# Edge blocks taken singly, and the last chunk's dense layers split at the nodes of the last two blocks

## The chip, the cores and the metric

The kernel runs on one core of a Trainium2 chip. The metric is the device time of one execution in microseconds. Five engines work beside each other, each through its own list in order: TensorE (PE; its weight loads are shown as PEld), VectorE (DVE), ScalarE (ACT), GpSimd (POOL) and SyncE (SP), which issues most of the plain transfers.

## The reference

A graph layer over 8,192 nodes with 256 channels and 131,072 edges, all in float32; the edges are sorted by their destination.

```python
ea = edge_attr @ w_e + b_e                       # 131072 x 64 @ 64 x 256
msg = relu(x[src] + ea)                          # gather of rows of x
agg = segment_sum(msg, dst, num_segments=8192)
t = x + agg
h_local = bn1(relu(t @ w1 + b1) @ w2 + b2 + x)
# attention of 4 heads within groups of 32 nodes, on x alone
h_attn = bn2(attention(x) @ out_w.T + out_b + x)
out = h_local + h_attn
out = out + relu(out @ m_w1 + m_b1) @ m_w2 + m_b2
result = layernorm(x + bn3(out))
```

The attention does not need the edges. The dense layers of a node need the sums of all edges that end in it.

## The kernel before, in words

**Edges.** The edges go in 128 blocks (NB) of 1,024. For a block, `gather` (L157) issues eight indirect transfers on POOL, each fetching 128 rows of x into a tile xs; there are four xs buffers. `edge_products` (L208, with the bias at L203 for the first 20 blocks) multiplies the edge attributes by w_e on PE. `edge_messages` adds both on DVE (L229) and applies relu on ACT (L233); the addition frees the xs buffer. `edge_hot` (L241) makes one-hot rows on DVE. `edge_sums` (L255) multiplies the one-hot rows by the messages, which gives the sums over a window of 32 nodes for each of four groups h of a block, each in its own 32 rows of the PSUM tile pw; they are copied to the tile ws (L265; for the last block L262 on DVE and L263 on ACT). `edge_place` (L280) multiplies ws by a second one-hot matrix, which puts the sums at their nodes in the PSUM tile l2, and DVE adds l2 to the transposed nodes xT (L289). The tiles pw and l2 share one buffer.

A block's window begins at node b x 64 minus a slack and is 64 nodes plus twice the slack wide; the slack is 24 at block 125 and 16 at blocks 126 and 127.

**Nodes.** The nodes go in 16 chunks of 512. `attention_front` and `attention_back` (L434 to L529) do the attention, with q and k at L445, scores at L476, the product with bd at L514 and the output projection at L526. `dense` does the four dense layers through its helper `layer` (L545), evacuated at L552 (w1, ACT), L555 (w2, DVE), L561 (m_w1, ACT) and L570 (m_w2, DVE), then transposes back (L582), adds x (L585), normalizes (L587 to L595) and stores (L598). A whole chunk's layers are 512 columns wide. The last two chunks go in parts: chunk 14 in two of 256, chunk 15 as 256, 128 and 128, each part with its own bound on which blocks must have been placed.

**Order.** PE's list is the order in which the program is written. A loop takes two blocks at a time up to block 103 (TAIL = 104): products and messages of the first, sums of the pair before, products and messages of the second, then the placement, and between them `work.run(us)`, which takes steps from four streams of node work (attention back and front, two of dense), each step with a planned cost, until its budget of 4.2 us (5.1 from block 20) a block is used up. A stream's entry may start when its condition holds; for dense this is `summed`: all blocks that reach into its nodes are placed. Up to block 25 the lists of DVE and ACT are in program order too; behind that a scheduler orders them. From block 104 on, a planner goes by times: `came` is when a block's gathers should have landed, and at each point it writes down whatever is due first of placement, sums, products, messages or a step of node work.

Of the kernel before, what the change touches and what calls it, by code (L numbers as in the profile page):

```python
# [72 lines left out]
def gnn_kernel(ctx: ExitStack, tc: tile.TileContext, x, src, dst, edge_attr, w, out):  # L73
# [173 lines left out]

    def edge_sums(blocks):

        pw = pps.tile([P, 2, C], FP, name="pw", tag="pw", bufs=1)  # L250
        for i, b in enumerate(blocks):
            msg, oh = msg_of.pop(b), oh_of.pop(b)
            turns = [(h, j) for j in range(TJ) for h in range(NH)]
            for h, j in sorted(turns) if b == NB - 1 else turns:
                nc.tensor.matmul(  # L255
                    pw[h * WN : (h + 1) * WN, i, :], oh[:, h * TJ + j, :], msg[:, h, j, :],
                    start=(j == 0), stop=(j == TJ - 1), skip_group_check=True,
                )
        n = len(blocks)
        ws = epool.tile([P, 2, C], FP, name="ws", tag="ws", bufs=2)  # L260
        if blocks[-1] == NB - 1:
            nc.vector.tensor_copy(ws[:, :n, :P], pw[:, :n, :P])  # L262
            nc.scalar.copy(ws[:, :n, P:], pw[:, :n, P:])  # L263
        else:
            newest["ws"] = nc.scalar.copy(ws[:, :n], pw[:, :n]).ins  # L265
        oh2 = epool.tile([P, 2, WB], FP, name="oh2", tag="oh2")
        for i, b in enumerate(blocks):
            wn = window(b)
            nc.vector.tensor_scalar(oh2[:, i, :wn], iota_n[:, :wn], wrow[:, b : b + 1], None, ALU.is_equal)
        return blocks, ws, oh2  # L270

    def edge_place(blocks, ws, oh2):
# [4 lines left out]
        for i, b in enumerate(blocks):  # L277
            at, wn = first_node(b) - n, window(b)
            for k in range(KC):
                nc.tensor.matmul(  # L280
                    l2[:, k, at : at + wn], ws[:, i, k * P : (k + 1) * P], oh2[:, i, :wn],
                    start=(i == 0 and k == 0), stop=(i == last), skip_group_check=True,
                )
# [250 lines left out]

    def dense(n0, st, pool, bank, t_a=0, t_z=TN, own=("h1", "m1", "zT", "y", "")):

        assert st["done"]
        nt = t_z - t_a
        cs, ts, part = slice(t_a * P, t_z * P), slice(t_a, t_z), nt / TN
        xn, tT, hA = st["xn"][:, ts, :], st["xT"][:, :, cs], st["hA"][:, :, cs]  # L540

        def layer(wt, nk, o, act):
            ps = bank()[:, : nt * P]
            for k in range(nk):
                nc.tensor.matmul(  # L545
                    ps, wt[:, k, o * P : (o + 1) * P], act[:, k, :], start=(k == 0), stop=(k == nk - 1)
                )
            return ps

        h1 = pool.tile([P, KC, nt * P], FP, name="h1", tag=own[0])  # L550
        for o in range(KC):
            nc.scalar.activation(h1[:, o, :], layer(w1, KC, o, tT), AF.Relu, bias=v_("b1", o))  # L552
            yield 1.7 * part
        for o in range(KC):
# [3 lines left out]
            yield 1.7 * part  # L558
        m1 = pool.tile([P, 2 * KC, nt * P], FP, name="m1", tag=own[1])
        for o in range(2 * KC):  # L560
            nc.scalar.activation(m1[:, o, :], layer(mw1, KC, o, hA), AF.Relu, bias=v_("m_b1", o))  # L561
            yield 1.7 * part
        zT = pool.tile([P, KC, nt * P], FP, name="zT", tag=own[2])
        for o in range(KC):

            nc.scalar.activation(
                zT[:, o, :], hA[:, o, :], AF.Identity, scale=s3[:, o : o + 1], bias=c3[:, o : o + 1]
            )
        for o in range(KC):
            nc.vector.scalar_tensor_tensor(  # L570
                zT[:, o, :], layer(mw2, 2 * KC, o, m1), s3[:, o : o + 1], zT[:, o, :], op0=ALU.mult, op1=ALU.add
            )
            yield 3.4 * part
        y = pool.tile([P, nt, C], FP, name="y", tag=own[3])
        st6 = pool.tile([P, TN, 6], FP, name="st", tag="st" + own[4])
        mv = pool.tile([P, TN, 2], FP, name="mv", tag="mv" + own[4])
        for t2 in range(0, nt, 2):
            n2 = min(2, nt - t2)
            ps = bank()[:, : n2 * C].rearrange("p (t c) -> p t c", t=n2)
            for t in range(n2):  # L580
                for k in range(KC):
                    nc.tensor.transpose(  # L582
                        ps[:, t, k * P : (k + 1) * P], zT[:, k, (t2 + t) * P : (t2 + t + 1) * P], ident
                    )
            nc.vector.tensor_add(y[:, t2 : t2 + n2, :], ps, xn[:, t2 : t2 + n2, :])  # L585
        for t in range(nt):
            nc.vector.bn_stats(st6[:, t, :], y[:, t, :])  # L587
            nc.vector.bn_aggr(mv[:, t, :], st6[:, t, :])
        rstd = pool.tile([P, TN], FP, name="rstd", tag="rstd" + own[4])
        nc.scalar.activation(rstd[:, :nt], mv[:, :nt, 1], AF.Sqrt, bias=eps_t)  # L590
        st["dense"] = t_z == TN
        yield 0.9 * part
        nc.vector.reciprocal(rstd[:, :nt], rstd[:, :nt])
        for t in range(nt):
            nc.vector.tensor_scalar(  # L595
                y[:, t, :], y[:, t, :], mv[:, t, 0:1], rstd[:, t : t + 1], ALU.subtract, ALU.mult
            )
        nc.sync.dma_start(out[ds(n0 + t_a * P, nt * P), :].rearrange("(t p) c -> p t c", p=P), y)  # L598
        yield 0.0
# [100 lines left out]
    with tc.manual_schedule(engines={PE}):  # L700

        def last_of(c, t_z=TN):

            return max(b for b in range(NB) if first_node(b) < c * CH + t_z * P)

        def summed(c, t_z=TN):
            last = last_of(c, t_z)
            return lambda: placed >= last and chunk[c].get("done") and not xp_of and b > 2

        for c in range(NCH):  # L710
# [11 lines left out]
            if c < NCH - 2:  # L722
                work.add(DENSE, summed(c), dense(c * CH, st, npool, bank))
        for i, c, t_a, t_z in (
            (DENSE2, NCH - 2, 0, 2), (DENSE, NCH - 2, 2, 4), (DENSE2, NCH - 1, 0, 2), (DENSE, NCH - 1, 2, 3),
            (DENSE2, NCH - 1, 3, 4),
        ):
            d = dense(c * CH, chunk[c], npool, bank, t_a, t_z, *([OTHER] if i == DENSE2 else []))
            ready = summed(c, t_z)
            if i == DENSE2:  # L730
                ready = lambda r=ready: r() and chunk[NCH - 1].get("done")
            work.add(i, ready, d)
# [5 lines left out]
        b = 0  # L738
        while b < TAIL:
            if b == NV:  # L740
                early.close()
                stated[0] = False
            blocks, per = range(b, b + 2), 2 * (PER_X if b < NX else PER)
            copying[0] = copy_stream(b // 2 - 1)
            for i in blocks:
                if i + 2 < NB:
                    gather(i + 2)
                if 4 <= i < 8:
                    wt, name = ((w1, "w1"), (w2, "w2"), (mw1, "m_w1"), (mw2, "m_w2"))[i - 4]
                    nc.sync.dma_start(wt, w[name].rearrange("(k p) m -> p k m", p=P))  # L750

            if b:
                edge_products(b)
                edge_messages(b)
                next_edges(b + 2)
            if waiting:
                sums = edge_sums(waiting)
            waiting = list(blocks)
            if not stated[0]:
                work.run(0.2 * per)  # L760
            edge_products(b + 1)
            edge_messages(b + 1)
            next_edges(b + 3)
            if stated[0]:
                for i in blocks:
                    edge_hot(i)
                    copy_some(2)
            work.run((0.3 if stated[0] else 0.1) * per)
            copy_load(b // 2)
            if sums:  # L770
                edge_place(*sums)
                placed, sums = sums[0][-1], None
            work.run(0.2 * per)
            if not stated[0]:
                for i in blocks:
                    edge_hot(i)
            work.run(0.5 * per)
            copy_some(4 * TN)
            b += 2

        came = [7.9 + 10.035 * (i + 1) for i in range(NB)]
        t, p, m, s, l = came[b - 2] + 20, b, b, b - 2, b - 2
        added = dict((i, came[i] + 2.0) for i in range(b))
        summed_at, bank_free = {}, t
        work.at = [t] * len(work.streams)
        while l < NB:
# [4 lines left out]
            elif s < m:  # L791
                times[1] = max(added[s] + 1.2, bank_free)
            if p < NB and m == p:
                times[2] = added[p - 1]
            if m < p:
                times[3] = came[m]
            if t >= times[0]:
# [3 lines left out]
                bank_free = work.placed_at = t + 0.7  # L801
                l += 1
            elif t >= times[1]:
                sums = edge_sums([s])
                t += 1.2
                summed_at[s] = t
# [146 lines left out]
```

## Time and profile before

| what | value |
|---|---|
| median of 3 runs | 1314.89 us (1314.71 to 1315.25) |
| profiled execution, whole | 1315.3 us |
| its span, first to last instruction | 1313.3 us |
| granted TensorE clock, mean | 0.959 |
| busy: PE, DVE, ACT, POOL | 1196.5, 800.9, 589.2, 976.1 us |
| rows of PE | 7,635 |
| gathers (L157) from x, from the copy xb | 160, 864 |

The profile is a page and a trace of one execution. In a group's row the numbers stand for: count, busy time in us, mean ns of one instruction, idle time of the engine just before them and what ended most of it. A timeline row gives start, length, engine, line, operation, tiles, shape and count. A wait's row gives who waited for whom, us in total, how often, and the longest. In a row of busy time by stretches, each engine's busy us is followed by the number of its instructions, and at the end stand granted clock, DMA share and GB/s.

### The profile page before, as it was taken

The numbers are of one execution on the slowest core, as the hardware profiler recorded it, in microseconds if no ns is written. First come the engines' busy times: TensorE is split into PE (matmuls) and PEld (weight loads), VectorE is DVE, ScalarE is ACT, GpSimd is POOL, SyncE is SP. The second block draws the span as 40 slices with busy tenths as digits, with TensorE's granted clock in tenths as the row PEclk, the third lists the DMA queues.
The fourth block names the chain that finished last, engine by engine and source line by source line (L and its number), as shares of the span: only waits on it lengthen the run. The fifth ranks groups of instructions, "written<-read, shape, count | busy, mean of one in ns | idle before, by whom it ended". The sixth has DMA issues, their size and how long they took to land.

```text
span 1313.3 us, 20960 instructions
## 1 busy us (share of the span) xinstructions
PE 1196.5 (91%) x7635; PEld 720.4 (55%) x7635; DVE 800.9 (61%) x1629; ACT 589.2 (45%) x841; POOL 976.1 (74%) x1032
## 2 busy tenths in 40 slices
PE   4987989999999989898997998989898999989987
PEld 3554655556555655554554554545556555555655
DVE  5567665756666565745646574565647558475754
ACT  2524443454545363544544444353454445444433
POOL 6777777777777777777777777777777777777772
PEclk8988999999999989998998998989898999999989
DMA  9999876677766665755757566576567567655742
GB/s 234 283 338 273 263 210 175 172 183 193 177 170 170 169 183 162 195 155 157 194 157 185 154 185 168 154 186 170 170 169 189 149 169 193 162 162 161 193 129 58
DMA packets 148905, 240.34 MB, mean 183 GB/s; under 512 B 27934, under 2 KB 112188, under 8 KB 148028
## 3 DMA queue, kind: packets, MB, share of 16 engines
q0 software_dynamic: 49152, 134.28, 38.0%
q1 hardware_dynamic: 98556, 104.65, 29.5%
q8 instruction: 62, 1.02, 0.3%
q14 instruction: 47, 0.39, 0.1%
q10 hardware_dynamic: 1088, 0.00, 0.0%
HBM read 222.06 MB, written 16.78 MB: 182 GB/s over the span
## 4 chain that ended last, share of the span: by engine, by line
PE 49%; POOL 20%; issue 10%; DMA 9%; DVE 7%; ACT 4%; SPq 0%; DVEq 0%; POOLq 0%; ACTq 0%
POOL xs L157 20%; PE at L545 13%; PE pe L208 10%; PE at L445 6%; DMA xs<-xb,srci 5%; PE pw L255 5%; PE at L526 3%; PE l L280 3%; PE pe L203 2%; DVE msg L229 2%; PE at L459 2%; DMA xs<-in_x_dram,srci 2%; PE at L514 1%; ACT pr L486 1%; DVE bd L506 1%
## 5 line engine op out<-in xcount | busy, mean ns | idle before, releaser
L157 POOL DMA_INDIRECT xs<-xb,srci x864 | 820.7, 950 | 263.4 <-issue 245.1
L233 ACT ACTIVATE msg<-msg 128x1024 f32<-128x1024 f32 (+1 forms) x259 | 270.0, 1046 | 402.6 <-DVE msg L229 398.6
L229 DVE TENSOR_TENSOR msg<-pe,xs 128x1024 f32<-128x1024 f32 (+1 forms) x259 | 306.5, 1205 | 196.0 <-PE pe L208 75.8
L208 PE MATMUL pe<-we,eaT 64*128 64x256 f32 x2048 | 267.8, 398 | 17.0 <-ACT pr L486 11.8
L208 PEld LDWEIGHTS pe<-we,eaT 64*128 64x128 f32 x2048 | 193.6, 192 | 121.2 <-issue 62.7
L157 POOL DMA_INDIRECT xs<-in_x_dram,srci x144 | 138.3, 961 | 43.9 <-issue 39.9
L255 PE MATMUL pw<-msg,oh 128*32 128x256 f32 x2048 | 128.8, 384 | 1.4 <-ACT msg L233 1.0
L545 PE MATMUL at<-hA,mw 128*128 128x512 f32 (+2 forms) x304 | 124.8, 538 | 3.4 <-DVE hA L555 3.4
L445 PE MATMUL at<-xT,inT 128*128 128x512 f32 x256 | 121.9, 602 | 3.2 <-ACT xT L435 3.2
L545 PE MATMUL at<-m,mw 128*128 128x512 f32 (+2 forms) x304 | 119.0, 534 | 0.1
L190 DVE STREAM_TRANSPOSE eaT<-ea 128x512 f32<-128x512 f32 x128 | 89.9, 702 | 24.7 <-PE pe L208 20.7
L255 PEld LDWEIGHTS pw<-msg,oh 128*32 128x32 f32 x2048 | 59.5, 110 | 63.3 <-issue 22.9
L280 PEld LDWEIGHTS l<-oh,ws 128*128 128x128 f32 x512 | 74.4, 196 | 28.1 <-issue 20.9
L280 PE MATMUL l<-oh,ws 128*128 128x160 f32 (+4 forms) x512 | 86.3, 309 | 2.4 <-ACT ws L265 1.6
L545 PEld LDWEIGHTS at<-hA,mw 128*128 128x128 f32 x304 | 54.1, 192 | 51.6 <-issue 40.8
L545 PEld LDWEIGHTS at<-m,mw 128*128 128x128 f32 x304 | 54.6, 192 | 48.7 <-issue 44.9
L445 PEld LDWEIGHTS at<-xT,inT 128*128 128x128 f32 x256 | 46.9, 191 | 57.5 <-issue 48.3
L448 ACT ACTIVATE qk<-at,vec 128x512 f32<-128x512 f32 x64 | 43.9, 685 | 74.9 <-PE at L445 74.8
L545 PE MATMUL at<-xT,w 128*128 128x512 f32 (+2 forms) x152 | 68.5, 588 | 7.4 <-DVE xT L289 7.4
L545 PE MATMUL at<-h,w 128*128 128x512 f32 (+2 forms) x152 | 65.0, 550 | 9.6 <-ACT oT L521 6.3
L561 ACT ACTIVATE m<-at,vec 128x512 f32<-128x512 f32 (+2 forms) x76 | 46.8, 618 | 56.5 <-PE at L545 56.2
L570 DVE SCALAR_TENSOR_TENSOR zT<-at,s,zT 128x512 f32<-128x512 f32 (+2 forms) x38 | 25.1, 662 | 72.0 <-PE at L545 72.0
(113 smaller groups left out, 1228.3 us busy)
## 6 DMA issues: line engine op xcount, KB each, us to landing
ea<-in_edge_attr_dram SPq DMA_DIRECT2D x512, 128.0 KB
xs<-xb,srci POOLq DMA_INDIRECT x864
xn<-in_x_dram SPq DMA_DIRECT2D x16, 512.0 KB
out_dram<-y SPq DMA_DIRECT2D x14, 512.0 KB
xp<-in_x_dram SPq DMA_DIRECT2D x10, 512.0 KB
xb<-xp SPq DMA_DIRECT2D x10, 512.0 KB
xp<-in_x_dram SPq DMA_DIRECT2D x3, 1024.0 KB
xb<-xp SPq DMA_DIRECT2D x3, 1024.0 KB
```

Source lines behind the costliest of these rows:

```text
L157: nc.gpsimd.indirect_dma_start(out=xs[:, h, j, :], out_offset=None, in_=x if b < NX else xb[:, :], in_offset=bass.IndirectOffsetOnAxis(ap= ...
L190: nc.vector.transpose(eaT, ea[:, QR:].rearrange("p (g d) -> p g d", d=ED)[:, :, :QR])
L208: nc.tensor.matmul(pe[:, i, u, :], eaT[rows, h + u], we[rows, :], start=(b >= NX), stop=True, skip_group_check=True)
L229: nc.vector.tensor_add(msg[:, hs, js].rearrange("p u i c -> p i u c"), pe[:, js, u : u + n, :], xs[:, hs, js].rearrange("p u i c -> p i u c"),
L233: nc.scalar.activation(msg[:, hs, js], msg[:, hs, js], AF.Relu)
L255: nc.tensor.matmul(pw[h * WN : (h + 1) * WN, i, :], oh[:, h * TJ + j, :], msg[:, h, j, :], start=(j == 0), stop=(j == TJ - 1), skip_group_ ...
L280: nc.tensor.matmul(l2[:, k, at : at + wn], ws[:, i, k * P : (k + 1) * P], oh2[:, i, :wn], start=(i == 0 and k == 0), stop=(i == last), ski ...
L445: nc.tensor.matmul(ps, inT[:, k, o * P : (o + 1) * P], xT[:, k, :], start=(k == 0), stop=(k == KC - 1))
L448: nc.scalar.activation(qk[:, o, :], ps, AF.Identity, bias=v_("in_b", o))
L526: nc.tensor.matmul(ps, outT[:, k, o * P : (o + 1) * P], oT[:, k, :], start=(k == 0), stop=(k == KC - 1))
L545: nc.tensor.matmul(ps, wt[:, k, o * P : (o + 1) * P], act[:, k, :], start=(k == 0), stop=(k == nk - 1))
L561: nc.scalar.activation(m1[:, o, :], layer(mw1, KC, o, hA), AF.Relu, bias=v_("m_b1", o))
```

## The change

The loop up to block 103 takes one block at a time; sums and placement of a block come one block later, not one pair later. The first two blocks are still summed together. Budgets for node work are the same per block. The order within an iteration of the first 26 blocks is: products, messages, sums of the block before, one-hot rows, 0.3 of the budget, placement, 0.7 of the budget.

The last chunk's dense layers go in four parts: nodes 0 to 256, 256 to 368, 368 to 432 and 432 to 512 of the chunk. `dense` takes node bounds instead of tiles of 128; a part that doesn't start at a multiple of 128 loads its own rows of x into a tile xl.

The last block's sums are made in two steps: the first three groups (`first_sums`), and the fourth when its messages are there. Its two copies go to two tiles ws, one from DVE and one from ACT, instead of two halves of one.

```diff
+    def first_sums(b):
         pw = pps.tile([P, 2, C], FP, name="pw", tag="pw", bufs=1)
+        group_sums(pw, 0, b, [(h, j) for h in range(NH - 1) for j in range(TJ)])
+        return pw
...
+            group_sums(pw, 0, blocks[0], [(NH - 1, j) for j in range(TJ)])
+            for k, copy in enumerate((nc.vector.tensor_copy, nc.scalar.copy)):
+                half = epool.tile([P, 2, C], FP, name="ws", tag="ws", bufs=2)
+                copy(half[:, 0, :P], pw[:, 0, k * P : (k + 1) * P])
+                ws.append(half[:, :, :P])
...
-    def dense(n0, st, pool, bank, t_a=0, t_z=TN, own=("h1", "m1", "zT", "y", "")):
+    def dense(n0, st, pool, bank, a=0, z=CH, own=("h1", "m1", "zT", "y", "")):
+        if a % P:
+            xr = pool.tile([P, 1, C], FP, name="xl", tag="xl", bufs=2)
+            nc.sync.dma_start(xr[:w, 0, :], x[ds(n0 + a, w), :])
...
-            (DENSE2, NCH - 2, 0, 2), (DENSE, NCH - 2, 2, 4), (DENSE2, NCH - 1, 0, 2), (DENSE, NCH - 1, 2, 3),
-            (DENSE2, NCH - 1, 3, 4),
+        late, last = (first_node(b) % CH for b in (NB - 2, NB - 1))
+            (DENSE2, NCH - 2, 0, CH // 2), (DENSE, NCH - 2, CH // 2, CH), (DENSE2, NCH - 1, 0, CH // 2),
+            (DENSE, NCH - 1, CH // 2, late), (DENSE2, NCH - 1, late, last), (DENSE, NCH - 1, last, CH),
...
-        while b < TAIL:
-            blocks, per = range(b, b + 2), 2 * (PER_X if b < NX else PER)
+        for b in range(NV):
+            per = PER_X if b < NX else PER
+            gather(b + 2)
             if b:
                 edge_products(b)
                 edge_messages(b)
                 next_edges(b + 2)
-            if waiting:
+            if b > 1:
                 sums = edge_sums(waiting)
+                waiting = []
+            waiting.append(b)
+            edge_hot(b)
+            copy_some(2)
+            work.run(0.3 * per)
             if sums:
                 edge_place(*sums)
                 placed, sums = sums[0][-1], None
+            work.run(0.7 * per)
...
+        for b in range(NV, TAIL):
+            gather(b + 2)
+            edge_products(b)
+            edge_messages(b)
+            next_edges(b + 2)
+            sums = edge_sums(waiting)
+            waiting = [b]
+            work.run(0.3 * PER)
+            edge_place(*sums)
+            placed = sums[0][-1]
+            work.run(0.2 * PER)
+            edge_hot(b)
+            work.run(0.5 * PER)
...
-        t, p, m, s, l = came[b - 2] + 20, b, b, b - 2, b - 2
+        t, p, m, s, l = came[b - 2] + 20, b, b, b - 1, b - 1
...
+                if s == NB - 1:
+                    times[1] = max(came[s] - 0.4, bank_free) if first is None else came[s] + 1.2
...
+            elif t >= times[1] and s == NB - 1 and first is None:
+                first = first_sums(s)
+                t += 0.8
```

## The prediction

> **What bounds the kernel now.** I read the page's engine rows first: TensorE (PE) is busy for 91% of the span and GpSimd (POOL) for 74%, which seems to say PE. The waits of POOL correct that.
>
> ```profile
> POOL xs L157 <- issue: 292.2, 951, 2.6
> POOL xs L157 <- DMA xs<-xb,srci: 5.8, 19, 0.3
> ```
>
> All of POOL's gaps but one are 0.3 us; the 2.6 us one stands ahead of the first gather, and 0.30 + 0.95 us is simply what one indirect gather takes. The timeline of POOL gives the ends of the stream:
>
> ```profile
> 4.23 1.10 POOL L157 DMA_INDIRECT xs<-in_x_dram,srcd  x1 [2.63 <-issue]
> ...
> 1290.23 0.95 POOL L157 DMA_INDIRECT xs<-xb,srci  x1 [0.30 <-issue]
> ```
>
> 1,024 gathers from 4.23 to 1291.18 are 1.257 us each: POOL never waits for anybody. So nothing done to blocks 0 to 103 can shorten the kernel; it can only lengthen it, by making a gather wait for its buffer. What can be won lies behind the last gather: 1313.3 - 1291.2 = 22.1 us. That stretch I read in the chain that ended last and in the busy time by stretches:
>
> ```profile
> 1294.57 1.15 PE pw L255 x16
> 1296.39 0.70 PE l L280 x4
> 1297.11 0.34 DVE xT L289
> 1297.49 6.12 PE at L545 x52
> 1303.61 0.40 PE at L582 x2
> 1304.01 2.75 PE at L545 x24
> 1306.78 0.36 DVE zT L570
> 1307.18 0.34 PE at L582
> ```
>
> ```profile
> 1274.48:1289.43 14.95, 14.43 (x106) 10.61 (x105) 5.37 (x12) 6.51 (x11) 11.29 (x13) 1.00 0.37 106
> 1289.43:1297.49 8.06, 5.29 (x45) 3.96 (x45) 6.00 (x18) 4.55 (x12) 1.45 (x2) 1.00 0.25 79
> 1297.49:1307.50 10.01, 9.68 (x80) 9.06 (x80) 3.62 (x11) 4.36 (x12) 0.00 (x0) 1.00 0.05 15
> ```
>
> (PE's busy time is the second number.) PE is full from 1274.5 to 1289.4, has 2.8 us idle around the last two blocks, and is full again from 1297.5 to the end: at full clock (1.00) the dense layers of the last chunk, not the edge sums, set the end.
>
> **What a narrow pass costs.** The change makes the parts 256, 112, 64 and 80 nodes wide instead of 256, 128 and 128 (blocks 126 and 127 begin at nodes 8,048 and 8,112, that is 368 and 432 within the chunk). A float32 multiplication leaves two rows in the trace; I call them passes. The groups kept apart by shape show what width is worth (mean ns behind the comma):
>
> ```profile
> L280 PE MATMUL l<-oh,ws 128*128 128x160 f32 x320 | 56.3, 321 | 0.0
> L280 PE MATMUL l<-oh,ws 128*128 128x144 f32 x80 | 13.2, 298 | 0.0
> L280 PE MATMUL l<-oh,ws 128*128 128x128 f32 x56 | 8.6, 284 | 0.5 <-ACT ws L265 0.5
> L280 PE MATMUL l<-oh,ws 128*128 128x112 f32 x40 | 6.1, 282 | 1.1 <-ACT ws L265 1.1
> L280 PE MATMUL l<-oh,ws 128*128 128x96 f32 x16 | 2.4, 283 | 0.8 <-ACT ws L263 0.8
> ```
>
> From 160 to 128 columns a pass gets 37 ns shorter, from 128 to 96 only 1 ns. So there is a floor at about 128 columns. The spacing at 128 columns comes from runs in the timeline: 8 passes take 1.06 us and 4 take 0.61, so (1.06 - 0.61)/4 = 0.112 us a pass; at 256 it is 3.04/14 = 0.217. I price 112, 80 and 64 columns at 0.112 us (the last two are an extension of the flat rows). Bounds: 0.112 above; below, in proportion from the 256-column row, 0.053 for 64 and 0.068 for 80. I take the upper end, since the 96-column row is the nearest.
>
> The Trainium skill, "TensorE: Matmul & The Clock Gate", section "LDWEIGHTS (loading the stationary operand)", says that a weight load takes its columns divided by 1.2 in ns, whatever the rows: 107 ns for the 128 columns that all these passes have. By that rule the floor is 0.107 and the sum below would be 0.5 us smaller. Its section "Back-to-back issue gap" gives an isolated 64-column matmul some 60 cycles; the 96-column row above speaks against using that here; by it the time would be that of the rival on width.
>
> **The change, part by part.**
>
> *Blocks 0 to 103 singly.* Each block gets its own pw copy, placement and xT addition; matmuls stay the same in number, ACT gets 50 more copies of about 0.4 us and DVE as many more short additions, both on engines busy 45% and 61%. None of it reaches the end unless POOL stops. The closest call is block 14, whose additions free the buffer of block 18 (four xs buffers):
>
> ```profile
> 185.70 1.22 DVE L229 TENSOR_TENSOR msg<-pe,xs 128x1024 f32<-128x1024 f32 x1 [0.50 <-PE pe L208]
> 187.28 0.95 POOL L157 DMA_INDIRECT xs<-in_x_dram,srci  x1 [0.30 <-DVE xp L621]
> ```
>
> The addition ends at 186.92 and the 145th gather starts at 187.28: 0.4 us to spare (blocks 10, 16 and 18 have 3.5). PE's order in the changed program puts 3.0 us more ahead of block 14's products: one block's sums and placement (1.3) and two output multiplications (1.7). Five times before that block a placement follows its sums at once, and must wait for the copy behind both relus, ready 2.7 us after the products (68.88 to 71.71 less 0.2 for a half-wide copy around block 4) while the sums cover 0.9: 5 x 1.8 = 9 us. Against that, the attention's bd now stands a block ahead of its use in DVE's order, so PE's two long waits on it (6.35 us at 83.5, 3.3 behind block 13) should go, and the 5.46 us wait at 117.6, where DVE had a whole softmax between two blocks, should shrink. Sum: 3.0 + 9 - 9.65 = +2.4, down to -3.1 if the last goes too. Less the 0.4 to spare, POOL stops for 0 to 2.0 us; if no wait goes, up to 11.6. I take 0, and keep the rest as a rival. From block 26 on the spare time is 17 us or more, so nothing there counts.
>
> *A fourth part.* One part is 24 multiplications, 48 passes x 0.112 = 5.4 us of PE, and two more transposes, 0.2; the 112-column part costs what a 128-column one did. +5.6 us, in a stretch where PE had 2.8 us idle.
>
> *When the last placement comes.* Products of block 126 start at 1274.48, held by a gather's landing, as before. Until the placement of block 126 (1288.35 before) PE now also does both first layers of the 112 part, 16 passes = 1.8 us, and waits 0.6 us for the xT addition right behind the placement of block 125, where second-layer work stood before: about 1290.7. DVE's additions of block 127 stand behind that block's xT addition, so they start at 1291.65 instead of 1289.29, and run without gaps (0.6 us for each of three, 0.35 for each of two): the last relu ends near 1294.8 instead of 1293.89. The sums of the first three groups end at 1295.1, a pair of 112-column multiplications takes 0.45, and the last group starts at 1295.55. Here the split saves nothing: its four passes share one column group and follow each other, and the whole block's 16 passes took 1.09 us because four groups run side by side. They end at 1296.6. The two copies into separate tiles run side by side: 0.45 instead of 0.75 us. The placement starts at 1297.1 instead of 1296.39, +0.7. Bounds: 1295.5 (if nothing but the last relu holds it) and 1297.4.
>
> *Behind the last placement.* The program's order has 38 multiplications and 4 transposes there before, 60 (12, 24 and 24 of the three parts) and 6 after. The 80-column part's first layer, ready at the xT addition, stands behind 26 of them. 0.45 for the placement + 120 passes x 0.112 = 13.4 + 0.4 for four transposes + 0.7 for the last zT step (1306.47 to 1307.18 before) = 15.0 us, so the last transpose starts at 1312.1 instead of 1307.18: +4.9 us. Normalization and store behind it are the same (6.1 us). The three earlier stores and the two small xl loads ride on SP, which is idle enough.
>
> Sum: 1315.3 (the profiled execution, 2.0 over its span) + 4.9 = 1320.2; it stood 0.4 above the median, so **1319.7**. With the placement's bounds and half a microsecond of waits the forecast's own range is 1317.6 to 1320.5.
>
> **Rivals.**
> - *POOL stops in the first 26 blocks*, on top of the tail: for it the 0.4 us at block 14, against it the vanishing bd waits. 1 to 3 us more: 1321 to 1323; 1331 at the outside.
> - *Passes cost by width* (it isn't slower): 24 x 0.096 + 48 x 0.053 + 48 x 0.068 = 8.1 us behind the placement, against 76 x 0.112 = 8.5. What remains is the later placement (+0.7) and up to 1.4 us of waits, since layers this short no longer cover the 0.7 us from a pass to its evacuated tile: 1315.2 to 1317. It decides if a 64-column pass is under 0.08 us.
> - *PE's idle 2.8 us takes up half of the new part*: +1.5 to 2.5, about 1317.
> - *The change does what its parts are for* (placement at 1295.5 and passes by width, without waits): -1.3, 1313.6. Even this is within 0.2%.
>
> **Chances.** Forecast 0.55, POOL stop 0.22, width 0.14, idle 0.04, the rest, faster, 0.05. Slower by over 0.2% (2.6 us, about what a measurement of this kernel can tell from no change) 0.77; within 0.18; faster 0.05. The range reaches from the width rival to the POOL stop: 1316.0 to 1323.0.
>
> **What would show it.** POOL's waits: no gap over 0.3 us (else the first rival). 64- and 80-column rows of the dense line with a mean near 282 ns, as at 128. The last placement near 1297, and some 126 PE rows behind it without gaps. The prediction is wrong if those rows are clearly shorter, if the 80-column part's first layer is done before 1299, or if the span ends under 1315.

## The result, and the profile after

The changed kernel takes 1328.68 us (median of 4 runs, 1328.38 to 1332.66) against 1315.07 for the kernel before in the same comparison: ratio 1.011, 95% interval 1.009 to 1.0129. It is slower by 13.6 us; the prediction was 1319.7, with a range that ended at 1323.0.

The profiled execution has a span of 1326.5 us (1313.3 before), 13.2 more. The first place to look is where the gathers end. First POOL's waits, then its timeline at two places:

```profile
POOL xs L157 <- issue: 292.9, 954, 2.6
POOL xs L157 <- DVE msg L229: 10.3, 13, 6.1
```

```profile
176.26 0.95 POOL L157 DMA_INDIRECT xs<-in_x_dram,srci  x1 [0.30 <-issue]
183.34 0.94 POOL L157 DMA_INDIRECT xs<-in_x_dram,srci  x1 [6.13 <-DVE msg L229]
...
1296.20 0.95 POOL L157 DMA_INDIRECT xs<-xb,srci  x1 [0.30 <-issue]
```

A gap of 6.1 us stands where before had none over 0.3: the first gather of block 17 waits for the additions of block 13, which free its buffer. The last gather is done at 1297.15 instead of 1291.18: 6.0 us of the 13.2 are this stop (a second and short one, 0.78 us, follows ahead of block 18's first gather). The other 7.2 us lie behind the last gather (29.4 us instead of 22.1). The chain that ended last shows them from the last block's sums on:

```profile
1299.98 2.25 PE pw L250 x12
1302.22 0.63 PE at L562 x4
1302.85 0.99 PE pw L250 x4
...
1303.87 0.30 DVE ws L274
...
1304.19 0.28 ACT ws L274
...
1304.51 0.69 PE l L290 x4
1305.20 4.44 PE at L562 x40
...
1319.60 0.32 PE at L599
```

The same stretch in busy time (span's length, then PE's busy time):

```profile
1299.00:1305.20 6.20, 4.66 (x28) 2.64 (x27) 4.49 (x14) 3.33 (x9) 0.00 (x0) 1.00 0.01 3
1305.20:1320.00 14.80, 14.42 (x126) 13.87 (x125) 6.83 (x24) 6.62 (x20) 0.00 (x0) 1.00 0.08 27
```

Three things are seen. The sums of the last block now take 2.25 + 0.99 us of TensorE in two pieces, where 16 passes took 1.15 before. The two copies still follow each other (1303.87, 1304.19). Behind the placement TensorE runs 126 rows without gaps, and the last transpose starts 15.1 us behind it; 15.0 was predicted. The narrow passes cost what was assumed; groups kept apart by shape (mean ns behind the comma):

```profile
L562 PE MATMUL at<-m,mw 128*128 128x112 f32 x16 | 2.2, 280 | 0.0
L562 PE MATMUL at<-m,mw 128*128 128x80 f32 x16 | 1.9, 275 | 0.0
L562 PE MATMUL at<-m,mw 128*128 128x64 f32 x16 | 2.1, 274 | 0.0
```

**Why POOL stopped.** In front of the gap, PE, then ACT, and then the last addition of block 13 on DVE, first in before and then in after, read:

```profile
168.63 5.28 PE L455 MATMUL at<-xT,inT 128*128 128x512 f32 x8 [6.64 <-ACT xT L445]
173.74 0.61 PE L290 MATMUL l<-oh,ws 128*128 128x128 f32 x4
...
178.09 1.13 PE L203 MATMUL pe<-be,sel 64*128 64x512 f32 x4
```

```profile
165.64 2.19 ACT L233 ACTIVATE msg<-msg 128x1024 f32<-128x1024 f32 x2 [7.14 <-DVE msg L229]
167.73 0.35 ACT L268 COPY ws<-pw 128x256 f32<-128x256 f32 x1
167.98 0.59 ACT L445 COPY xT<-at 128x512 f32<-128x512 f32 x1
```

```profile
165.60 1.23 DVE L229 TENSOR_TENSOR msg<-pe,xs 128x1024 f32<-128x1024 f32 x1 [0.50 <-PE pe L208]
...
181.85 1.22 DVE L229 TENSOR_TENSOR msg<-pe,xs 128x1024 f32<-128x1024 f32 x1 [0.50 <-PE pe L208]
```

The copies that TensorE needs next (ws, and xT for the attention) stand in ScalarE's list behind both relus of block 12, whose additions VectorE made late (164.39 to 166.74) because a softmax stood ahead of them. TensorE stands in line meanwhile, and block 13's products come at 178.09, so that its additions end at 183.07. In before they ended at 166.83, 10.4 us ahead of the gather that waits for them (177.28), because the products of block 13 stood in PE's list close behind those of block 12, the first of the pair, with only the sums of the pair before between them. Taken singly, the second block of a pair loses this lead, and block 13 has no more to spare than block 14.

How late PE is shows at block 14, the one that the prediction counted: its additions end at 193.54 instead of 186.92, 6.6 us later. The waits ahead of its products are those between 60 and 190 us, of which these are the longest, first in before and then in after:

```profile
PE at L514 <- DVE bd L506: 8.5, 2, 6.3
...
PE l L290 <- ACT ws L268: 12.4, 6, 3.3
```

In after the rows give 12.4 us for the copy ws, 6.6 for xT and 1.4 for others, 20.4 in all; before had 17.9 (8.5 for bd, 5.5 behind DVE's additions, 3.2 for xT, 0.7 for scores). That is 2.5 us of waits more, on top of the 3.0 us of work ahead of the products that the prediction counted: 5.5 of the 6.6.

My first theory: (a) the stop comes from the copy ws behind the relus in the first 26 blocks; (b) the tail is late because of the fourth part, and because its products of block 126 start 1.06 us late. Rivals: the stop comes from VectorE's softmax whatever the order; or from single blocks anywhere; the tail's loss comes from the split points holding up the placement of block 126, or from the split sums.

### The profile page after: what moved, and what is told of

It reads as the page before. It is cut to its first block, busy times and chain, and to the rows that moved or that the text cites. A ratio compares the mean times of both kernels' runs of the same rounds, so it can differ in the third digit from the quotient of the medians.

```text
span 1326.5 us, 21314 instructions
## 1 busy us (share of the span) xinstructions
PE 1206.5 (91%) x7685; PEld 715.5 (54%) x7685; DVE 819.0 (62%) x1688; ACT 598.6 (45%) x904; POOL 976.0 (74%) x1032
## 4 chain that ended last, share of the span: by engine, by line
PE 46%; POOL 19%; DVE 11%; issue 10%; DMA 9%; ACT 4%; SPq 1%; DVEq 0%; ACTq 0%; POOLq 0%
POOL xs L157 19%; PE at L562 14%; PE pe L208 9%; PE at L455 5%; DMA xs<-xb,srci 5%; PE pw L250 4%; DVE msg L229 4%; PE l L290 3%; PE at L536 3%; PE pe L203 2%; PE at L469 2%; DMA ea<-in_edge_attr_dram 2%; PE at L524 2%; ACT msg L233 2%; ACT pr L496 1%
## 5 line engine op out<-in xcount | busy, mean ns | idle before, releaser
L250 PE MATMUL pw<-msg,oh 128*32 128x256 f32 x2048 | 142.7, 389 | 3.3 <-ACT msg L233 3.2
L290 PE MATMUL l<-oh,ws 128*128 128x160 f32 (+4 forms) x512 | 93.1, 305 | 40.4 <-ACT ws L268 36.0
L562 PE MATMUL at<-hA,mw 128*128 128x512 f32 (+4 forms) x320 | 126.3, 521 | 3.3 <-DVE hA L572 3.3
L290 PEld LDWEIGHTS l<-oh,ws 128*128 128x128 f32 x512 | 77.7, 192 | 95.2 <-ACT ws L268 58.3
L562 PE MATMUL at<-m,mw 128*128 128x512 f32 (+4 forms) x320 | 119.6, 517 | 0.0
L190 DVE STREAM_TRANSPOSE eaT<-ea 128x512 f32<-128x512 f32 x128 | 89.9, 702 | 30.0 <-PE pe L208 26.8
L250 PEld LDWEIGHTS pw<-msg,oh 128*32 128x32 f32 x2048 | 55.3, 110 | 75.8 <-issue 36.0
L299 DVE TENSOR_TENSOR xT<-l,xT 128x320 f32<-128x320 f32 (+9 forms) x157 | 60.6, 401 | 53.2 <-PE l L290 52.4
L578 ACT ACTIVATE m<-at,vec 128x512 f32<-128x512 f32 (+4 forms) x80 | 48.0, 600 | 79.0 <-PE at L562 78.4
L241 DVE TENSOR_TENSOR oh<-iota_n,rel 128x128 f32<-128x128 f32 x256 | 60.3, 275 | 23.4 <-PE pw L250 23.3
L562 PE MATMUL at<-xT,w 128*128 128x512 f32 (+4 forms) x160 | 72.6, 587 | 2.1 <-DVE xT L299 2.1
```

The source lines that it names most:

```text
L190: nc.vector.transpose(eaT, ea[:, QR:].rearrange("p (g d) -> p g d", d=ED)[:, :, :QR])
L241: nc.vector.tensor_tensor(oh[:, ts], iota_n[:, None, :WN].to_broadcast([P, TB // 2, WN]), rel[:, b, ts, None].to_broadcast([P, TB // 2, WN ...
L250: nc.tensor.matmul(pw[h * WN : (h + 1) * WN, i, :], oh_of[b][:, h * TJ + j, :], msg_of[b][:, h, j, :], start=(j == 0), stop=(j == TJ - 1), ...
L290: nc.tensor.matmul(l2[:, k, at : at + wn], ws[k][:, i, :], oh2[:, i, :wn], start=(i == 0 and k == 0), stop=(i == last), skip_group_check=True,
L299: newest["xT"] = nc.vector.tensor_add(xT, l2[:, :, a - n : z - n], xT).ins
L562: nc.tensor.matmul(ps, wt[:, k, o * P : (o + 1) * P], act[:, k, :], start=(k == 0), stop=(k == nk - 1))
```

## The experiments

Each is compared with the kernel before on the same chip, whose median was 1315.84, 1318.00 and 1315.61 us for runs 1 to 4, 5 to 8 and 9 to 11. "Behind" is the time from the end of the last gather to the end of the span in the profiled execution (before 22.1, after 29.4).

**1. The old loop with the new tail.**

```diff
-        for b in range(NV):
+        while b < TAIL:
...
-        t, p, m, s, l = came[b - 2] + 20, b, b, b - 1, b - 1
+        t, p, m, s, l = came[b - 2] + 20, b, b, b - 2, b - 2
```

> The loop of before (blocks 0 to 103 in pairs) with the tail of after (four parts, first_sums). Theory (the stop of GpSimd comes from the single blocks alone, the late end from the tail alone): no gap of GpSimd over 0.4 us, last gather done near 1291.2; the tail costs 6.1 to 7.2 us: 1321.2 if the 1.06 us by which the products of block 126 start too late come from the single blocks, 1322.3 if they come from the tail's own order. Rival (the tail is late because the stop upset the planner's times): 1315 to 1319.

Ratio 1.0047 (1.0032 to 1.0063), 6.2 us. No gap over 0.3, last gather done at 1289.5, behind 29.8. So the tail's loss is there without single blocks.

**2. The new loop with the old tail** (the kernel before, with the loop of after).

```diff
-        while b < TAIL:
+        for b in range(NV):
...
+        for b in range(NV, TAIL):
...
-        t, p, m, s, l = came[b - 2] + 20, b, b, b - 2, b - 2
+        t, p, m, s, l = came[b - 2] + 20, b, b, b - 1, b - 1
```

> The loop of after (blocks singly) with the tail of before (three parts of 256, 128 and 128, all sums of the last block after its last message). Theory: the first gather of block 17 waits about 6.1 us for the additions of block 13, last gather done near 1297.2, tail as before: 1321.1; 1322.2 if the single blocks also start the tail 1.06 us late. Rival (stop and tail belong together): 1315, or 1328.

Ratio 1.0083 (1.0055 to 1.0111); behind 23.3, last gather done at 1300.6. The stop is there without the new tail, and in this execution it cost 9.4 us, not 6.0: POOL has gaps of 2.8, 6.1 and 0.8 us ahead of the first gathers of blocks 16, 17 and 18, where after has 6.1 and 0.8 ahead of 17 and 18. PE's waits between 60 and 190 us are the same as in after (12.4, 6.6 and 1.4 us). The difference lies in the first 60 us: the granted clock from 20 to 60 us was 0.87 (0.96 in the profile of after), a DMA that TensorE waits for came 0.7 us later, and the additions of block 13 end at 186.5 instead of 183.1. The 3.4 us more there are the 3.4 us more at the end (1300.59 against 1297.15): with no time to spare, each microsecond that TensorE loses ahead of block 13 reaches the end.

**3. Pairs to block 25, single blocks from 26 on, new tail.**

```diff
-        while b < TAIL:
+        while b < NV:
...
+        for b in range(NV, TAIL):
+            gather(b + 2)
...
```

> Pairs up to block 25, single blocks from 26 to 103, the tail of after. Theory (only the first 26 blocks can stop GpSimd, since 17 us are to spare from block 26 on): no gap of GpSimd over 0.4 us, and the time of the kernel with pairs throughout and the new tail, 1321.2 to 1322.3. Rival (single blocks stop GpSimd wherever they stand): near after, 1327 to 1329.

Ratio 1.0048 (1.003 to 1.0067), as in run 1; no gap over 0.3. The rival falls: 78 single blocks from 26 on cost nothing. This run also took a part of my own theory away. Its products of block 126 start 16.68 us ahead of the last gather's end, as in before (16.70; after 15.63), and behind it are 29.35 us all the same: the 1.06 us late start does not reach the end.

**4. The sums and their copy ahead of the next messages**, in the first 26 blocks of after.

```diff
                 edge_products(b)
-                edge_messages(b)
-                next_edges(b + 2)
             if b > 1:
                 sums = edge_sums(waiting)
                 waiting = []
+            if b:
+                edge_messages(b)
+                next_edges(b + 2)
```

> After, with one change in the first 26 blocks: the sums of block b-1 and the copy of their result are issued ahead of the additions and relus of block b, so that the copy on ScalarE no longer stands behind those relus. Theory (TensorE loses its time at placements that wait for this copy): its idle time before placements for the copy falls from 36 us to under 15, the 6.1 us gap ahead of block 17's first gather goes, 1322.7. Rival (VectorE's softmax between two blocks' additions makes them late, whatever the order of the copy): a gap of 4 to 6 us stays, 1326.5 to 1328.7.

Ratio 1.0042 (1.0027 to 1.0056), 5.5 us: the stop is gone (no gap over 0.3; at block 17 2.3 us to spare), the tail's part is left (behind 29.3). PE's waits over the whole span, first after, then this run:

```profile
PE l L290 <- ACT ws L268: 36.0, 22, 3.3
...
PE at L455 <- ACT xT L445: 6.6, 1, 6.6
```

```profile
PE l L290 <- ACT ws L268: 26.2, 22, 3.2
...
PE at L455 <- ACT xT L445: 8.6, 3, 7.6
```

The sum fell by 10 us, not to under 15 as I had written, because only the first 26 blocks were changed: between 60 and 190 us it fell from 12.4 to 2.9. The long wait for xT that stands right in front of the stop is still there, and longer (7.6). The additions of block 13 end 8.0 us sooner than in after (175.06), and those of block 11, ahead of that wait, are sooner by as much already (146.10 against 154.07). So it was not the last wait before the gap that decided, but the small ones ahead of it. VectorE's softmax alone does not stop POOL.

**5. Four parts, the last sums in one go** (run 1's kernel without first_sums; copies, and the planner's times for the last messages, as before).

```diff
-            elif t >= times[1] and s == NB - 1 and first is None:
-                first = first_sums(s)
-                t += 0.8
...
-                times[3] = came[m] - (2.4 if m == NB - 1 else 0.0)
+                times[3] = came[m]
```

> Blocks in pairs, four parts as in after, but the last block summed in one go behind its last message, with the copies as before. The measure is the time from the end of the last gather to the end of the span (before 22.1 us, after 29.4, pairs with the new tail 29.8). Theory (the split of the last sums costs time: twelve passes wait on TensorE for the relus, then a dense layer and four passes in series stand ahead of the copies): 28.3 to 29.2. Rival (the split is worth what it is meant to save): 30 or more. If neither, 29.3 to 29.9: then the fourth part is nearly all of it.

Ratio 1.0037 (1.0023 to 1.0051), 4.9 us; behind 27.1. The last sums of this run in PE's timeline:

```profile
1298.64 1.09 PE L250 MATMUL pw<-msg,oh 128*32 128x256 f32 x16
```

1.09 us instead of 3.30 (2.25 + 1.05 in the same view). The time behind the last gather is under every range that I had written. The split sums cost about 2 us in the profiles (29.3 to 29.8 against 27.1); the two ratios say 1.3, with intervals that overlap. The last placement starts 8.4 us behind the last gather here, a microsecond later than in after (7.4), and the end still comes sooner.

**6. Three parts with the split sums** (pairs).

```diff
-            (DENSE, NCH - 1, CH // 2, late), (DENSE2, NCH - 1, late, last), (DENSE, NCH - 1, last, CH),
+            (DENSE, NCH - 1, CH // 2, 3 * P), (DENSE2, NCH - 1, 3 * P, CH),
```

> Blocks in pairs, the three parts of before (256, 128, 128), the split sums and the two copies into separate tiles as in after. From the last gather to the end of the span: theory (the fourth part costs 48 narrow passes at 0.112 us and two transposes, 5.6 us, and the split sums 0.3 to 0.9): 22.4 to 23.0. Rival (the split sums make most of the loss): 25 to 29. If the split saves time: 21.4 to 22.0.

Ratio 1.0007 (0.9997 to 1.0017), 0.9 us, not told apart from before; behind 24.95, of which 1.6 us are a granted clock of 0.78 from 1270 to 1280 us, ahead of the products of block 126. From there to the end of PE's work it takes 34.0 us, before 33.0. Without the 1.6 us it would be some 23.35 behind, by my estimate: the split sums alone are not most of the loss, but they cost somewhat more than I had expected (22.4 to 23.0).

**7. Split at 368 alone** (256, 112, 144; pairs, old sums).

```diff
+            (DENSE, NCH - 1, CH // 2, late), (DENSE2, NCH - 1, late, CH),
```

> Blocks in pairs, last sums as before, three parts of 256, 112 and 144: only the first of the two new split points. From the last gather to the end: theory (a part costs its passes, width below 128 is worth nothing): no part is added, the last has 48 passes at about 0.123 us with little beside them to cover its evacuations: 21.3 to 22.8, so within 1 us of before. Rival (the early start that the split points give is itself what hurts, by holding the placement of block 126 up): 23.5 to 26.

Ratio 1.0024 (1.0013 to 1.0035), 3.2 us; behind 27.1, with a granted clock of 0.79 in the 8 us ahead of the last gather's end (products 3.05 us instead of 2.00). Here the rival was nearer the truth, though 27.1 lies above its range too. No pass is added, yet the placement of block 126 comes 2.6 us behind the last gather instead of 2.8 ahead. The 112 wide part's early layers delay the last m layer of the 256 wide part until its relu on ScalarE stands behind the message relus of block 126; TensorE waits 1.80 us for it. The additions of block 127, behind that placement in VectorE's list, start at +3.6 instead of -1.9. How much of the 3.2 us each of these makes was not separated.

**8. Split at 432 alone** (256, 176, 80; pairs, old sums).

```diff
+            (DENSE, NCH - 1, CH // 2, last), (DENSE2, NCH - 1, last, CH),
```

> Blocks in pairs, last sums as before, three parts of 256, 176 and 80: only the second of the two new split points. From the last gather to the end: theory: the same 24 multiplications a part as before, the 176 wide ones at about 0.15 us a pass instead of 0.112 (1.8 us more in all), part of it in TensorE's idle time: 22.1 to 23.5. Rival (passes cost by width, so that the 80 wide part is short): 20 to 21.5.

Ratio 1.0008 (0.9994 to 1.0022), 1.1 us. Its 48 passes of 176 columns took 8.3 us of PE, the 48 of 80 columns 5.5. The profiled execution (behind 27.1) had a granted clock of 0.65 from 1270 to 1280 us and began the products of block 126 2.5 us late; from there it took 34.6 us against 33.0. The rival on width falls: 48 passes of 80 columns in 5.5 us are 0.115 us each, not 0.068. The 27.1 us lie outside what I had expected (22.1 to 23.5), and 2.5 of them are that late start.

**9. The 112 wide part held back** until block 126 is placed (pairs, new tail).

```diff
-            ready = summed(c, z)
+            ready = summed(c, z + (c == NCH - 1 and z == late))
```

> Pairs with the new tail, but the 112 wide part may start only behind the placement of block 126, as the second part of before did. Theory (started early, its layers push the fourth m relu of the 256 wide part behind the message relus of block 126 on ScalarE, TensorE waits 0.85 us for it and the placement of block 126 comes 4 us late): the placement of block 126 goes back from 1.2 us behind the last gather to 2 to 3 us ahead of it and that wait goes; but the passes are the same in number and only move behind the last placement, so the end gains little: 27.5 to 29.3 us from the last gather to the end, against 29.8. Rival (the late placement of block 126 is what makes the tail late): 25 to 26.

Ratio 1.0045 (1.003 to 1.0061); behind 29.3. The placement of block 126 went back to 2.4 us ahead of the last gather's end, and the last one to +4.9 (after +7.4), yet the end moved by less than 0.6 us. With four parts, when the placements come hardly matters: TensorE has the same passes to run, before or behind them.

**10. Single blocks with the order of run 4, and the old tail** (run 2's kernel with run 4's edit).

```diff
+            if b > 1:
+                sums = edge_sums(waiting)
+                waiting = []
             if b:
-                edge_products(b)
                 edge_messages(b)
```

> Single blocks as in after, with the sums of block b-1 and their copy issued ahead of the messages of block b in the first 26 blocks, and the tail of before. Theory (the two places found are all that the change costs): no gap of GpSimd over 0.4 us, 22 to 23.3 us from the last gather to the end, within 1.5 us of before. Rival (single blocks cost something more, for instance through the tail's first blocks): 3 us or more slower.

Ratio 1.0007 (0.9991 to 1.0023): with the two places undone, the rest of the change costs nothing that can be told. No gap over 0.3. The profiled execution was 26.8 us behind, outside what I expected, and the busy time by stretches shows why:

```profile
1296.00:1303.00 7.00, 6.53 (x29) 6.29 (x30) 0.68 (x2) 1.77 (x5) 0.00 (x0) 0.50 0.00 0
```

The granted clock was 0.50 in these 7 us.

**11. Before, with two edits in the tail.**

```diff
-                times[1] = max(added[s] + 1.2, bank_free)
+                times[1] = max(added[s] + (0.3 if s == NB - 1 else 1.2), bank_free)
...
-        if blocks[-1] == NB - 1:
-            nc.vector.tensor_copy(ws[:, :n, :P], pw[:, :n, :P])
-            nc.scalar.copy(ws[:, :n, P:], pw[:, :n, P:])
-        else:
-            newest["ws"] = nc.scalar.copy(ws[:, :n], pw[:, :n]).ins
+        newest["ws"] = nc.scalar.copy(ws[:, :n], pw[:, :n]).ins
```

A third edit, a sooner placement of block 126 in the planner's times, left the order there as it was.

> Before, with two small edits in the tail alone: the last block's sums ahead of the second first-layer pair of m (0.8 us with its wait, which then fills the time behind the placement), and one copy of the sums by ScalarE (0.37 us for 128x256 in the row of before) in place of two that run one after the other (0.29 and 0.27). Theory: last placement 0.6 to 0.9 us sooner, the end 0.2 to 0.8 sooner: 21.3 to 21.9 us behind the last gather, not to be told from before in the time. Rival (TensorE's work behind the placement simply grows by what was moved): 22.1 to 22.4.

1314.11 us, ratio 0.9985 (0.9975 to 0.9995): some 2 us faster than before by the ratio, 1.5 by the medians, where I had expected no difference that can be told. Behind the last gather are 21.45 us, 0.7 less than before; the rest of the difference is not explained by these edits, and which of the two gave the 0.7 us was not separated. PE's timeline, then the copy in ACT's:

```profile
1291.85 1.81 PE L255 MATMUL pw<-msg,oh 128*32 128x256 f32 x16
1294.12 0.69 PE L276 MATMUL l<-oh,ws 128*128 128x96 f32 x4 [0.46 <-ACT ws L261]
```

```profile
1293.70 0.37 ACT L261 COPY ws<-pw 128x256 f32<-128x256 f32 x1 [0.32 <-PE pw L255]
```

From the last sum to the placement PE now waits 0.46 us, where it waited 0.79 for two copies.

## Why the prediction was wrong, step by step

**The POOL stop at nothing: wrong, and the larger part of the miss** (6.0 of 9.0 us). The mechanism was named as a rival, with its cause (copies behind both relus), its waits and its kind of price; what failed was the step "Sum: 3.0 + 9 - 9.65 = +2.4 ... POOL stops for 0 to 2.0 us ... I take 0". The terms against measurement, between 60 and 190 us: waits for the copy ws 9 predicted, 12.4 measured, in six waits instead of five; the wait for xT not counted, 6.6 against 3.2 before; the bd waits did go, as said, but they were 8.5 us and not 9.65 (of the 3.3 behind block 13, 1.1 were waits for xT); the 5.5 us one went too, by which the sum would have been -3.1. With 0.7 of other waits PE lost 5.5 us there instead, and 0.4 was to spare. I set a credit of 9.65 us, whose place in the list I had not followed to its end, against a debit, and took the better end of what was left. The stop also came one block sooner, at block 13: I had looked for the least time to spare in the order of pairs, where block 13 has 10.4 us, and not in the new order, where it has none. Run 2 adds that even 6.0 is one draw: it was 9.4 there.

**Blocks 26 on cost nothing: right** (runs 3, 10).

**A narrow pass costs 0.112 us: right.** From 112 to 64 columns a row has 280, 275 and 274 ns. The four-part run 3 spent 5.2 us of TensorE on 48 passes of 64 columns, 0.108 each. The rival on width is out. By the Trainium skill, "TensorE: Matmul & The Clock Gate", section "LDWEIGHTS (loading the stationary operand)", it is the 128 weight columns that take the time, 107 ns; the spacing of the passes agrees within 1 to 5 ns. No run here changes the number of weight columns, so the floor is measured and its reason is the page's.

**The tail, +4.9: too small by 1.5.** Counted from the products of block 126 to the last transpose, before takes 33.0 us (29.4 busy, 3.6 idle) and run 3 39.5 (36.3 and 3.2). The 6.4 us more, with each row counted from the end of the one before it, are: dense layers, transposes included, +4.9 (13.3 before in passes of 128 columns, 18.1 now); sums +2.2 (3.0, 5.2 now); the rest and the idle time -0.7. The fourth part's 5.6 stands up, less 0.7 saved elsewhere in these rows. The missing term is the split sums, which I had put at nothing in TensorE's time: I saw that the fourth group alone takes 1.05 us, but not that the first twelve passes, written ahead of their relus, hold TensorE for 2.25 us while they wait for them one group after the other. Run 5 shows it by taking them away, though the planner's times for the last messages changed with them. The 1.05 us itself was right: four passes into one column group (32 weight columns) took 1.05 us, and 16 passes spread over four groups 1.09.

In the prediction's own steps the error stands in the last placement: put at 5.9 us behind the last gather (1297.1) and at most 6.2, it came 7.4 behind it, +2.2 where +0.7 was written. But the step itself was the wrong way to count: the last placement came at +8.4 in run 5 and at +4.9 in run 9, and the end moved by 2 us the other way in the one and by under 0.6 in the other. By these two runs what sets the end is how long TensorE needs for everything from block 126 on, and that sum the prediction did not carry through.

**"The two copies run side by side": wrong.** They follow each other, as before (0.30 and 0.28, 0.02 apart), though they go to two tiles: both read the tile pw. In the trace ScalarE's copy is released by VectorE's. The Trainium skill, "PSUM — Partial Sum Buffer", section "PSUM bank collisions raise a hardware error", says that a scheduler makes two engines that touch the same bank and partitions wait for each other, reads too; the trace agrees that one waits for the other. No run tests whether the shared tile is the reason.

**The placement of block 126 at 1290.7: 1 us too soon.** It came 0.5 us behind the last gather instead of 0.5 ahead. In after, the way from the products of block 126 to it was as predicted (16.1 us), but those products started 1.06 us late, from a cause that stays open; in run 3 they start in time, and a wait of 0.89 us for a relu of m that stands behind message relus takes its place. Neither is seen in the end of this tail (runs 3 and 9). In run 7 such a wait was 1.80 us and may have cost some of the 3.2.

**Behind the last placement 15.0 us: right** (15.1). The remaining 0.8 us of the 13.2 lie behind TensorE's last row, 6.6 us instead of 5.8; the old tail of run 2 has 6.6 too, so the new tail need not be their cause, which stays open.

## What to carry to other kernels

Where a stage has no time to spare, count the waits of the whole stretch ahead of it in its new order, and take no credit for a wait that goes until the place it moves to has been read; a copy in a list behind the next block's long operations stalls whoever needs it, and moving its issue ahead of them gave the whole stop back. A part of a matrix product costs its passes, not its width, below the width where a pass stops getting shorter (about 128 columns here), so splitting finer only to start sooner has to be paid for by idle time of TensorE. Work written ahead of its data on an engine that runs in order does not start sooner: it holds the engine.

## What the runs showed that was not expected

The granted clock dips at different places in different executions of programs that are alike there. Read in slices of 1 us (runs 6, 7, 8, 10 and after, around their dips), it is 1.00 or 0.50, but for slices in which it changes; the means of 0.65 to 0.79 in runs 6 to 8 are such dips seen through a longer window. In run 7 the dip is 3.4 us long, in run 10 it is 10 us (1293 to 1303), and there the spacing of 128-column passes went from 0.112 to 0.213 us. This dip moved the end of the profiled span by some 3.5 us (26.8 us behind the last gather against 23.3 for the same tail in run 2), more than most of what is compared here, so small verdicts rest on medians.

The end of the gather stream, where POOL never waits, lay between 1289.5 and 1292.2 us from one kernel's profile to the next.
